# Projections of the next batch beside its first two score steps, and the weight shifts ten pieces later, in an attention and mixture-of-experts kernel

## The chip, the cores and the metric

The kernel runs on one core of a Trainium2 chip. The metric is the device time of one execution in microseconds (us); lower is better. The core has five engines that run their own instruction streams: TensorE (PE in the profile; its weight loads, PEld, are shown apart and overlap it), VectorE (DVE), ScalarE (ACT), GpSimd (POOL) and SyncE (SP), which here issues nearly all DMAs. Engines meet through semaphores; each executes its own stream in order, so an instruction that waits holds up all behind it.

## The reference, cut to what matters

The input x is 8 batches of 512 tokens of width 256. All is fp32.

```python
# attention, 16 heads of 16, causal; then residual and layer norm
q, k, v = split(x @ w_qkv);  a = softmax(mask(q @ k.T / 4)) @ v
x1 = layernorm(x + a @ w_out)
# feed-forward: top 6 of 16 experts by softmax(x1 @ gate_w.T) + gate_b
y = sum over chosen e of c[e] * (silu(x1 @ w1[e].T + b1[e]) * (x1 @ w3[e].T + b3[e]) @ w2[e].T + b2[e])
z = silu(x1 @ ws1.T + bs1) * (x1 @ ws3.T + bs3) @ ws2.T + bs2      # shared expert
out = layernorm(x1 + y + z)
```

## The kernel before, in words

**Batches and steps.** Each batch b goes through `attention(b)` (L332). Four first units prepare it: `transpose_x` (L337, 8 transposes on TensorE of the batch's tokens, tile x), `project_qk(0)` and `project_qk(1)` (L345, queries and keys of one half of the heads each) and `project_v` (L367). Then come 16 steps i, one for each of four query tiles q, two head halves m and two head parities s. Step i is in two parts: `front(i)` issues the score matmuls (sc, L399), whose results VectorE masks and reduces (L410) and GpSimd and ScalarE negate (L421, L426); `back(i)` turns the weights of step i-1 (transposes tp, L438, exponentials on ScalarE, L440) and adds up the weighted values of step i-2 (po, L447). So the pipeline is three steps deep, and two more units (16 and 17) empty it.

**Behind attention.** When a query tile is complete, `finish_tokens` (L478: output projection, residual, layer norm on VectorE), `transpose_tokens`, `gate`, `compare`, `place` and `send` follow at fixed distances of 3 to 15 pieces. `send` scatters the tokens on the GpSimd queue to the slots of their experts (xs). The shared expert of batch b is 7 units, `hidden` x3 and `collect` x4 (L655 to L712). `collect(t)` adds the shared result into the token tile x and then SyncE stores it (acc, L708).

**Groups.** Batches form three groups, (0,1), (2 to 5), (6,7). After the last batch of a group, `table(grp)` (L716) works out on VectorE which expert each tile of 128 slots belongs to, and then SyncE loads the ends of the experts from SBUF (L764) and issues 16 fills of the slots behind them (L772). `expert_units(grp)` (L795) then runs the routed experts a tile at a time; `fetch` brings the tokens (xg, L823), `up` and `down` are pab and py. Routed experts of one group run beside the attention of the next group.

**The order of the work.** It is written out by hand for TensorE, VectorE and ScalarE (`manual_schedule`, L1022). `line` (L959) is a list of pieces; for every piece the loop at L1023 issues what was put off to it (`due`), its own function, what lies beside it (`beside`, filled by `put`: clears, weight shifts, tables, expert units) and last its `behind`, here `back(i)`. Before the change a batch takes 20 pieces: 16 steps, unit 16 with the next batch's `transpose_x`, unit 17 with the next batch's `project_qk(0)`, and two pieces with nothing but `project_qk(1)` and `project_v` (L983, L984). The shared units of the batch before stand beside steps 7 to 13, and `load_x(b + 2)` beside step 14 (L974, L987). Expert units are spread evenly over the pieces of a group's stretch (L1018 to L1021). SyncE and GpSimd are not ordered by hand; a scheduler places their instructions.

**Token tiles.** `load_x` (L90) fills a tile from a pool of two. The load for batch b+2 writes into the tile of batch b, so it waits until the scatters of b have read it and until all four acc stores of b have read it. `transpose_x` of batch b+2 waits for the load; on TensorE everything behind it waits too.

**Weight shifts.** `shift_weights(e)` (L256) loads a correction for two experts (352 KB, L259, a pool of two buffers) and two and three pieces later adds it to the resident expert weights on VectorE (L263), 16 additions in all, from piece 22 on (L1006). The first routed expert runs at piece 63 before the change.

Of the kernel before, what the change touches and what calls it, by code (L numbers as in the profile page):

```python
# [31 lines left out]
def attn_moe_postln_kernel(  # L32
# [57 lines left out]
    def load_x(b):  # L90
        t = two.tile([P, NT, 2 * E + D], F32, tag="x", name=f"x_{b}")
        nc.sync.dma_start(out=t[:, :, 2 * E :], in_=x[b].rearrange("(t p) d -> p t d", p=P))
        xts[b] = t
# [162 lines left out]
    def shift_weights(e):  # L256

        c = two.tile([P, 2, 2 * EH], F32, tag="yg", name=f"shift_{e}")
        nc.sync.dma_start(out=c, in_=shift[e : e + 2].partition_broadcast(P))  # L259
        for i in range(2):  # L260
            w = wev[:, e + i, : 4 * EH].rearrange("p (c n) -> p c n", c=ND)
            ci = c[:, i].unsqueeze(1).to_broadcast([P, ND, 2 * EH])
            later(2 + i, lambda w=w, ci=ci: nc.vector.tensor_add(w, w, ci))  # L263
# [59 lines left out]
    def later(n, fn, last=False):  # L323
        due.setdefault(clock["now"] + n, ([], []))[last or n > 2].append(fn)
# [633 lines left out]
    parts = [attention(b) for b in range(B)]  # L958
# [5 lines left out]
    def add(fn, behind=nothing):  # L964
        line.append((fn, behind))
# [3 lines left out]
    rest = []  # L969
    for b in range(B):  # L970
        own = parts[b][1]
        for i, (fn, behind) in enumerate(own[:-2]):

            if i >= 7 and rest:  # L974
                add(lambda fn=fn, also=rest.pop(0): (fn(), also()), behind)
            else:
                add(fn, behind)

        nxt = parts[b + 1][0] if b + 1 < B else [nothing] * 4
        add(lambda a=own[-2][0], c=nxt[0]: (a(), c()), own[-2][1])  # L980
        add(lambda a=own[-1][0], c=nxt[1]: (a(), c()), own[-1][1])
        sent[b] = len(line) - 1 + 15
        add(nxt[2])  # L983
        add(nxt[3])  # L984
        rest = shared_units(b)
        if b + 2 < B:
            rest.append(lambda b=b: load_x(b + 2))  # L987
    for _ in range(14):
        add(nothing)
    for fn in rest:  # L990
# [7 lines left out]
    def put(at, fn):  # L998
        beside.setdefault(min(at, len(line)), []).append(fn)
# [3 lines left out]
        for i, b in enumerate(grp.batches):  # L1003
            put((sent[grp.batches[0]] if g else 30) + 12 * i, lambda b=b: clear(b))
    for e in range(0, E, 2):
        put(22 + e, lambda e=e: shift_weights(e))  # L1006
    for g, grp in enumerate(groups):
        put(starts[g], lambda grp=grp: table(grp))
        put(starts[g] + 2, lambda grp=grp: spread(grp))
# [83 lines left out]
```

## Time and profile before

| what | value |
|---|---|
| median of three runs | 1399.78 us (1398.6 to 1404.23) |
| the profiled execution: its own time | 1408.78 us |
| its span, first to last instruction | 1407.1 us |
| outside the span | 1.7 us |
| mean granted TensorE clock | 0.949 |
| busy: PE, POOL, DVE, ACT | 1310.7 us (93%), 890.1 (63%), 807.9 (57%), 713.5 (51%) |
| chain that ended last, by engine | PE 75%, DVE 8%, DMA 5%, SP's queue 4%, issue 3%, POOL 3%, ACT 2% |
| idle before scores' reduction e (L410), waiting for sc | 77.9 us of DVE |
| SP waiting for we_sb additions (L263) at L259 | 29.7 us |
| POOL waiting for the load of x at L370 | 15.4 us in 6 waits |

The page cuts the span in 40 slices of 35 us and gives the busy share of each in tenths, and in the row PEclk the clock that TensorE was granted. A view by windows gives the busy time of each engine, the clock and the DMA share in any stretch; the view in order of time gives each instruction's start and length, in square brackets the idle time just before it and what ended it. A matmul in fp32 is recorded as two instructions, so that four score matmuls show as x8.

### The profile page before, as it was taken

Reading aid. Unit: us, or ns where it says so; the run is one execution under the profiler, and the core shown is the slowest. Engines: PE = TensorE matmul, PEld = TensorE weight load, DVE = VectorE, ACT = ScalarE, POOL = GpSimd, SP = SyncE. Lnnn points to the kernel's source line nnn. Section 1 sums busy time; section 2 is a strip of 40 time slices with the busy share of each in tenths; the row PEclk is TensorE's granted clock in tenths of the full one; section 3 lists DMA queues with packets and bytes.
Section 4 is the critical chain, followed back from the end, with each engine's and each line's share of the span. In section 5 each row is a group of like instructions: output and inputs, shape, how many; then the busy total and the mean of one; then the engine's idle time right before and its main releaser. Section 6 shows DMA issues by size and latency. Waiting matters only on the chain.

```text
span 1407.1 us, 29371 instructions
## 1 busy us (share of the span) xinstructions
PE 1310.7 (93%) x8868; PEld 906.4 (64%) x8868; DVE 807.9 (57%) x2853; ACT 713.5 (51%) x1749; POOL 890.1 (63%) x1006
## 2 busy tenths in 40 slices
PE   7997998999999999999999999999989999999990
PEld 4564665666676577667756766677766765777770
DVE  3766967856664765666565844555534342255545
ACT  3442453454564455455555555555645554566660
POOL 3446647548656865775586557775567873577772
PEclk9995996999999999899999999999999999999995
DMA  9895211233223222333231345553456776587854
GB/s 279 230 348 175 69 53 51 72 105 84 62 54 88 56 68 65 72 76 68 56 89 45 102 103 96 94 113 68 83 107 131 136 146 130 125 157 167 176 120 138
DMA packets 184148, 156.73 MB, mean 111 GB/s; under 512 B 56109, under 2 KB 176570, under 8 KB 183994
## 3 DMA queue, kind: packets, MB, share of 16 engines
q1 hardware_dynamic: 140378, 100.51, 25.8%
q0 software_dynamic: 43344, 53.55, 21.2%
q8 instruction: 75, 1.23, 0.4%
q14 instruction: 79, 0.65, 0.2%
q10 hardware_dynamic: 272, 0.79, 0.1%
HBM read 66.08 MB, written 94.55 MB: 114 GB/s over the span
## 4 chain that ended last, share of the span: by engine, by line
PE 75%; DVE 8%; DMA 5%; SPq 4%; issue 3%; POOL 3%; ACT 2%; POOLq 0%; DVEq 0%; ACTq 0%; another core or an unknown queue 0%
PE pab L858 19%; PE py L878 14%; PE tp L438 8%; PE sc L399 5%; PE po L447 5%; PE tb L841 4%; PE tb L837 4%; PE qk L354 4%; PE pa L666 3%; SPq L311 3%; PE pb L666 2%; PE spy L698 2%; DVE e L410 2%; PE v L379 2%; PE pr L481 1%
## 5 line engine op out<-in xcount | busy, mean ns | idle before, releaser
L887 POOL DMA_INDIRECT sum<-y,yat x237 | 377.0, 1591 | 190.9 <-ACT y L886 112.2
L858 PE MATMUL pab<-we_sb,xgT 128*128 x936 | 325.6, 471 | 14.0 <-ACT xgT L848 8.1
L421 POOL TENSOR_SCALAR e<-e,nb 128x128 f32<-128x128 f32 (+3 forms) x384 | 222.1, 676 | 120.5 <-DVE nb L410 117.8
L410 DVE CUSTOM_DVE_ANT_0 e<-sc,none 128x512 f32<-128x512 f32 (+3 forms) x512 | 220.5, 485 | 84.9 <-PE sc L399 77.9
L878 PE MATMUL py<-we_sb,hT 88*128 (+1 forms) x948 | 249.8, 386 | 0.7 <-issue 0.5
L868 DVE SCALAR_TENSOR_TENSOR h<-h,pab 128x176 f32<-128x176 f32 x237 | 79.4, 335 | 279.8 <-ACT h L867 163.9
L878 PEld LDWEIGHTS py<-we_sb,hT 88*128 88x128 f32 (+1 forms) x948 | 183.4, 194 | 66.3 <-issue 5.0
L600 POOL DMA_INDIRECT xs<-x,idi x192 | 193.0, 1005 | 50.4 <-issue 44.7
L858 PEld LDWEIGHTS pab<-we_sb,xgT 128*128 128x128 f32 x936 | 162.7, 194 | 68.6 <-ACT xgT L848 9.7
L438 PE MATMUL tp<-ident,e 128*128 128x128 f32 x1280 | 183.5, 291 | 11.3 <-POOL e L421 5.2
L440 ACT ACTIVATE eT<-tp 128x512 f32<-128x512 f32 x320 | 170.7, 599 | 35.1 <-PE tp L438 30.7
L886 ACT ACTIVATE y<-py,yat 128x256 f32<-128x256 f32 x237 | 112.3, 474 | 132.3 <-PE py L878 98.3
L438 PEld LDWEIGHTS tp<-ident,e 128*128 128x128 f32 x1280 | 146.1, 147 | 45.3 <-issue 23.9
L399 PE MATMUL sc<-kT,qT 32*128 32x384 f32 (+3 forms) x1024 | 135.7, 511 | 9.6 <-DVE nb L410 7.4
L844 ACT COPY hT<-tb 88x256 f32<-88x256 f32 x237 | 87.2, 368 | 110.2 <-PE tb L841 85.5
L426 ACT ACTIVATE e<-e,nb 128x128 f32<-128x128 f32 (+3 forms) x128 | 71.2, 556 | 128.7 <-DVE nb L410 111.2
L867 ACT ACTIVATE h<-pab 128x176 f32<-128x176 f32 x237 | 75.1, 317 | 104.6 <-PE pab L858 82.2
L848 ACT ACTIVATE xgT<-tb,ident 128x256 f32<-128x256 f32 x234 | 110.9, 474 | 6.3 <-PE tb L841 2.1
L447 PE MATMUL po<-eT,v 128*32 128x128 f32 x2560 | 102.8, 289 | 11.1 <-DVE t L471 7.2
L447 PEld LDWEIGHTS po<-eT,v 128*32 128x32 f32 x2560 | 64.2, 112 | 56.3 <-issue 34.7
L837 PE MATMUL tb<-ident,h 128*88 128x128 f32 x474 | 92.8, 277 | 1.4 <-PE cnt L561 0.5
L841 PE MATMUL tb<-ident,xg 128*128 128x128 f32 x468 | 90.3, 275 | 3.5 <-DMA xg<-xs 3.4
(148 smaller groups left out, 1593.9 us busy)
## 6 DMA issues: line engine op xcount, KB each, us to landing
xg<-xs SPq DMA_DIRECT2D x237, 128.0 KB
sum<-none SPq DMA_DIRECT2D x24, 512.0 KB
yg<-sum SPq DMA_DIRECT2D x96, 128.0 KB
we_sb<-in_w SPq DMA_DIRECT2D x6, 1408.0 KB
xs<-none SPq DMA_DIRECT2D x3, 2304.0 KB
xs<-none SPq DMA_DIRECT2D x48, 144.0 KB
x<-in_x SPq DMA_DIRECT2D x8, 512.0 KB
acc<-x SPq DMA_DIRECT2D x32, 128.0 KB
```

The lines of the kernel that those rows point to most:

```text
L399: nc.tensor.matmul(sc[:, :n], lhsT=qT[ts(r, 32), m, s, ts(q, P)], rhs=kT[ts(r, 32), m, :n], start=True, stop=True,)
L410: nc.vector.tensor_tensor_reduce(out=e[:, :n], in0=scs[r][:, :n], in1=mask[:, S - n :], scale=-0.25, scalar=BIG, op0=ALU.add, op1=ALU.min, ...
L421: nc.gpsimd.tensor_scalar(e[:, :n], e[:, :n], -1.0, nb[:, r : r + 1], ALU.mult, ALU.add)
L438: nc.tensor.transpose(tp[:, ts(r, P)], es[r][:, ts(k, P)], ident)
L440: nc.scalar.activation(eT, tp, AF.Exp)
L447: nc.tensor.matmul(po[ts(r, 32), s, :], lhsT=v2[:, k, 4 * m + r, s : s + 2, :].rearrange("p h i -> p (h i)"), rhs=eTs[k][:, ts(r, P)], sta ...
L600: d = nc.gpsimd.indirect_dma_start(out=grp.xs, out_offset=bass.IndirectOffsetOnAxis(ap=idi[:, k : k + 1], axis=0), in_=xts[b][:, t, :], in ...
L837: nc.tensor.transpose(tp[:HC, 2 + c, :], h[:, ts(c, HC)], ident)
L841: nc.tensor.transpose(tp[:, c, :], xg[:, ts(c, P)], ident)
L858: nc.tensor.matmul(pab, lhsT=xgT[:, c, :], rhs=we_sb[:, ds(e * WE + c * 2 * EH, 2 * EH)], start=(c == 0), stop=(c == ND - 1),)
L878: nc.tensor.matmul(py, lhsT=hT[: HC + c, c, :], rhs=we_sb[: HC + c, ds(e * WE + 4 * EH + c * D, D)], start=(c == 0), stop=(c == 1),)
L887: nc.gpsimd.indirect_dma_start(out=grp.sums[j % SUMS], out_offset=bass.IndirectOffsetOnAxis(ap=st["at", j][:, 0:1].bitcast(I32), axis=0), ...
```

## The change

A batch now takes 18 pieces. `project_qk(1)` and `project_v` of batch b (b over 0) no longer have pieces of their own; they are issued right behind the score matmuls of that batch's steps 0 and 1. The shared units move from steps 7 to 13 to steps 6, 7, 8 (`hidden`) and 12, 13, 14, 15 (`collect`), and `load_x(b + 2)` is issued with the last `collect`, at step 15 in place of 14. The weight shifts start at piece 32 in place of 22. What is counted from the end of a batch (the `due` distances, `sent`, and so `table` and the first expert units) keeps its distance in pieces; since the two pieces are gone, it falls two steps later in the next batch: `table` at step 14 in place of 12, `send` of the last query tile at steps 12 to 14 in place of 10 to 12.

```diff
         for i, (fn, behind) in enumerate(own[:-2]):
 
-            if i >= 7 and rest:
+            if b and i < 2:
+                add(lambda fn=fn, also=parts[b][0][2 + i]: (fn(), also()), behind)
+
+            elif rest and (6 <= i < 9 or i >= 12):
                 add(lambda fn=fn, also=rest.pop(0): (fn(), also()), behind)
             else:
                 add(fn, behind)
...
         sent[b] = len(line) - 1 + 15
-        add(nxt[2])
-        add(nxt[3])
         rest = shared_units(b)
         if b + 2 < B:
-            rest.append(lambda b=b: load_x(b + 2))
+            rest[-1] = lambda b=b, fn=rest[-1]: (fn(), load_x(b + 2))
...
     for e in range(0, E, 2):
-        put(22 + e, lambda e=e: shift_weights(e))
+        put(32 + e, lambda e=e: shift_weights(e))
```

The compiled programs hold the same TensorE, VectorE, ScalarE and GpSimd work in another order; SyncE's DMAs are the same in number and size.

## The prediction

> **What bounds the kernel now.** I read the page first. TensorE is busy for 1310.7 of 1407.1 us and holds 75% of the chain that ended last. In the slices it is full except near the start and the end, and its clock drops to half twice near the start.
>
> ```profile
> PE   7997998999999999999999999999989999999990
> ...
> PEclk9995996999999999899999999999999999999995
> ```
>
> The fourth and seventh slices (105 to 140 and 211 to 246 us) are the first steps of batches 1 and 2. So I took the start of every score step from TensorE's instructions in order of time and asked the view by windows for steps 0 to 6 of each batch. Columns: stretch, length, busy PE, PEld, DVE, ACT, POOL, clock, DMA share, GB/s.
>
> ```profile
> 98.78:133.89 35.11, 22.60 (x152) 14.23 (x151) 25.95 (x104) 7.83 (x22) 23.04 (x35) 0.61 0.67 232
> 206.94:233.76 26.82, 21.84 (x151) 13.52 (x150) 20.86 (x96) 7.89 (x21) 20.92 (x35) 0.60 0.12 45
> 310.68:344.35 33.67, 32.27 (x213) 21.10 (x212) 24.42 (x109) 15.45 (x44) 26.06 (x38) 0.90 0.31 80
> 438.90:473.58 34.68, 31.53 (x224) 21.29 (x223) 24.87 (x108) 16.72 (x47) 29.51 (x40) 0.95 0.36 79
> 566.13:601.38 35.25, 32.66 (x224) 21.84 (x223) 24.81 (x108) 17.27 (x47) 29.99 (x39) 0.85 0.39 77
> 695.94:729.86 33.92, 31.59 (x224) 21.24 (x223) 24.49 (x107) 16.34 (x47) 28.63 (x38) 0.95 0.38 79
> 830.09:895.88 65.79, 62.63 (x379) 44.72 (x378) 33.73 (x140) 36.47 (x99) 53.16 (x58) 0.97 0.55 102
> ```
>
> Length less busy PE is the idle time: 12.5 us in batch 1, 5.0 in batch 2, then 1.4, 3.2, 2.6, 2.3, 3.2 (12.7) in batches 3 to 7. That is all that better cover in the first steps can win back, plus lost clock. The rest of each batch is TensorE-bound: in the window 310.70 to 438.90 us it is busy for 126.77 of 128.20 us. No matmul is removed, so the change pays only in waits, and any new wait of TensorE is paid in full.
>
> **Gains, part by part.** The weight shifts: the view in order of time shows VectorE stuck behind one load in batch 1:
>
> ```profile
> 119.61 0.89 DVE L263 TENSOR_TENSOR we_sb<-we_sb,shift 128x704 f32<-128x704 f32 x1 [5.69 <-DMA shift<-shift]
> ```
>
> TensorE waits 3.41 us for the division queued behind it. The load was issued at 106.6 us, while the clears and weight loads filled the DMA engines; ten pieces later that traffic is over, so the 3.4 us go. The 16 additions (0.89 us each in the median, 14 us) leave batch 1's early steps; some 7 of them, 6.2 us, arrive in steps 0 to 6 of batch 2, where VectorE is busy for 20.86 of 26.82 us and so has 6 us free: nearly full. The last addition comes at piece 49, the first expert at piece 61, so nothing routed waits for it.
>
> The projections: `project_qk(1)` took 3.70 us of TensorE, `project_v` 3.62 us, with nothing of their batch beside them. They now lie between the scores and the first transposes, where the waits for the chain reduction, negation, exponential stand (2.71 us on "DVE nb", 0.97 us on "POOL e" in batch 2). But they stand at steps 0 and 1 only; the waits of steps 3 to 6 stay, and the finishing work of the last query tile (about 3.5 us of VectorE) moves from steps 0 to 2 into steps 2 to 4. Bounds of the gain: nothing, and all the idle time. I take about half. Batch 1: 3.4, plus a third of the other 9.1, is 6.4 us. Batch 2: 2.5 less the additions, say 1. Batches 3 to 7: half of 12.7 is 6.3, and of the clock lost there ((1 - 0.90) x 33.7 + 0.05 x 34.7 + 0.15 x 35.3 + 0.05 x 33.9 + 0.03 x 65.8 = 14 us) a fifth, 3. Sum 16.7 us. Batches 1 and 2 without experts stay thin in steps 2 to 6, so I expect their clock to drop as now. The new copies of queries and values are the same instructions; on ScalarE they go ahead of step 0's last negation, and `project_v`'s 3.6 us of matmuls cover that; without this cover it would cost some 1 to 2 us a batch.
>
> **The cost: the load of the token tile.** This is the step I weigh most. Order on TensorE after the change, from the last `collect` (step 15) to the next batch's `transpose_x` (unit 16): counts, gate, at most one expert tile, po x32, tp x16, xp. In the trace of before the same stretch lasts 407.79 to 414.11 us, 6.3 us, with an expert tile, and 185.49 to 189.39, 3.9 us, without. Before, three steps lay between (`collect` at step 13).
>
> Against that stands the chain from the last spy matmul to the landed load. In the trace: VectorE adds (L706), SP stores (L708), the load (L92) is issued when that store has landed, and GpSimd's iota (L370) starts when the load has.
>
> ```profile
> 396.19 0.33 SPq L708 DMA_DIRECT2D acc<-x  x1
> 399.35 0.13 SPq L92 DMA_DIRECT2D x<-in_x  x1
> ...
> 404.30 0.19 POOL L370 IOTA x<- 128x64 int32 x1 [4.67 <-DMA yat<-xs]
> ...
> 414.11 1.04 PE L342 MATMUL xp<-ident,x 128*128 128x128 f32 x8
> ```
>
> The spy before it ended at 394.8, so the chain took 9.5 us; for the loads of batches 5, 6 and 2 it took 7.9, 8.7 and 8.5. Mean 8.7. Before, TensorE came to xp 15 to 20 us after spy, so nobody waited. Now it comes after 6.3 or 3.9.
>
> - Loads of batches 4, 5, 6 (an expert tile lies between): 8.7 - 6.3 = 2.4 each, 7.2 us. A rule of the Trainium skill gives less: "DMA: Bandwidth & Descriptors", section Anatomy of one DMA, puts a DMA at about 2.0 us plus its bytes at 436 GB/s, for the GpSimd path. By that the store (128 KB) is 2.3, the load (512 KB) 3.2, the chain with 1.4 us for the addition 6.9, and the stall 0.6 each. The trace has 1.9 to 3.2 and 4.0 to 5.4 for SP's own transfers beside other traffic; I take the trace.
> - Load of batch 2 (no expert tile): 8.7 - 3.9 = 4.8, plus a 352 KB weight shift that now stands just ahead of it on SP and waits for an addition of the same step; 0 to 3 us, I take 1. Sum 5.8.
> - Loads of batches 3 and 7: `table` now stands at step 14, and SP's order has the 16 fills ahead of the last store and of the load. In the trace:
>
> ```profile
> 274.52 0.15 DVE L758 SCALAR_TENSOR_TENSOR ends<-eio,run 1x16 int32<-1x16 f32 x1
> ...
> 275.98 9.37 SPq L772 DMA_DIRECT2D xs<-none  x15
> 285.45 0.39 SPq L708 DMA_DIRECT2D acc<-x  x1
> 287.37 0.39 SPq L92 DMA_DIRECT2D x<-in_x  x1
> ...
> 291.60 0.20 POOL L370 IOTA x<- 128x64 int32 x1 [1.30 <-DMA x<-in_x]
> ```
>
> From the ends to the landed load is 16.9 us, and the same from 784.8 to 801.7 for batch 7. Before, TensorE came to xp at 291.5 and 802.3: just in time, with `table` at step 12. Two steps later there is no slack. Step 14's reductions started 4.0 us after its scores on TensorE; with them, spy's addition and the table (2.5 + 0.4 + 3.5) the ends come 10.4 us after step 14's scores. TensorE needs 5.9 us from there to step 15's scores (sc 1.1, spy 1.4, x1p 0.4, po 1.0, tp 2.0), or 8.5 with an expert tile. So the ends come 4.5 us after step 15's scores in batch 2 and 1.9 in batch 6; the load lands at 21.4 and 18.8; xp is due at 1.1 + 1.4 + 3.9 = 6.4 and 8.8. Stalls 15 and 10 us; since VectorE may lag less, I take 14 and 10. The table's VectorE time falls in that shadow, which gives back about 3 us of waits in steps 13 to 15.
> - After two such stalls the clock may be cold. The one row for it is the start: after 7.06 us idle, xp took 1.94 us against 1.04, and 16 qk 8.13 against 7.30. That is 1.7 us a stall, 3.4 in all; at the least 0.
>
> Sum of costs: 7.2 + 5.8 + 24 + 3.4 = 40.4 us. Queued behind xp on TensorE are the output projection, po, the transposes of step 15 and `project_qk(0)`, so everything of the next batch waits; on SP the fetches of expert tokens queue behind the load, but they run three tiles ahead. The scatters of the old tile end well before (before: at step 10 to 12; now 12 to 14), so they aren't last.
>
> Expert tiles: the same number over 18 pieces a batch, 3.4 in place of 3.1 in a piece for the second group; TensorE-bound either way, 0. The tail after batch 7 keeps its order, 0, with 3 us of doubt either way.
>
> Net: 40.4 - 16.7 - 3 = 20.7 us slower. The profiled execution took 1408.78 us, 0.6% over the median of 1399.78; the difference is set against the median: 1420 us.
>
> **Rivals.** (a) The other side: the clock holds. If the dense projections at steps 0 and 1 keep TensorE at full clock through steps 2 to 6 of batches 1 and 2, then (1 - 0.61) x 35 + 0.40 x 27 = 24 us of lost clock come back besides the 17; with loads that land at the quick end (7.9) and smaller table stalls (8 each) the costs are 27. Then 1399.8 + 27 - 3 - 41 = 1383 us. It decides in favour of faster once batches 1 and 2 show a clock over 0.9 there. Against it: VectorE is 21 us busy in those steps without additions, so TensorE can't be dense. 7%. (b) No difference: stalls at the low end (27) against gains of 24 and the 3; 1400 us, 14%. (c) The stated cause, 1420 us, 65%. (d) Worse: the stalls leave the clock at half through the thin steps that follow, and the additions overload VectorE in batch 2; another 20 us, 1440, 14%.
>
> A measurement of this kernel can tell about 0.5%, 7 us, from no change. Faster 0.07, same 0.14, slower 0.79. The range reaches from the no-difference case to the worse one, 1399 to 1440 us.
>
> **What would show it.** TensorE idle before xp (L342) on the DMA of x: near 14 and 10 us for batches 3 and 7, 6 for batch 2, 2 to 3 for 4 to 6. The idle time in steps 0 to 6 down to 5 us in batch 1 and by half in batches 3 to 7, and no wait of L263 on the shift's load. I am wrong if xp doesn't wait, or if the clock of steps 0 to 6 in batches 1 and 2 rises above 0.9.

## The result, and the profile after

The changed kernel took 1473.67 us in the median of four runs (1471.05 to 1474.2), the kernel before beside it 1402.01 us: ratio 1.0508, interval 1.0475 to 1.054. The forecast was 1420 us with a range up to 1440: the direction was right, the size was not.

The page first, the two rows that were shown of before. The span is now 1471.7 us, so a slice is 37 us.

```profile
PE   7999979959999999899899969999999999999990
...
PEclk9998988879999999999999988999999999999995
```

The clock no longer falls to half in the early slices, but it stays at 8 and then 7 tenths in the sixth to ninth slice, where all but one were at 9 before; and PE has two slices at 5 and 6 tenths, the ninth (294 to 331 us) and the 24th (846 to 883), where batches 2 and 6 hand over to 3 and 7. Now the view by windows for steps 0 to 6 of batches 1, 2 and 4, with the columns of the earlier fence:

```profile
91.00:127.64 36.64, 32.20 (x197) 19.47 (x193) 21.76 (x103) 13.23 (x33) 21.84 (x37) 0.81 0.73 257
196.43:236.72 40.29, 32.90 (x197) 20.02 (x193) 27.06 (x109) 13.00 (x33) 22.96 (x37) 0.79 0.22 74
...
450.19:498.86 48.67, 44.97 (x280) 29.51 (x276) 28.71 (x121) 22.70 (x61) 31.52 (x43) 0.96 0.31 62
```

With 7.3 us more of projections in these steps, batches 1 and 2 hold a clock of 0.8 in place of 0.6. But length less busy PE is still 4.4 us in batch 1, and 7.4 and 3.7 us in batches 2 and 4, more than before. So I took the start of every step from TensorE's instructions in order of time and asked the view by windows for each stretch of batches 1 to 7. "Idle" is length less busy PE, "lost clock" is (1 - granted clock) x length; both in us, summed over the batches. Part of the time at a lower clock TensorE stood idle anyway, and that part would be counted twice. In brackets stands the clock lost while TensorE was busy, from the trace's clock records laid over its instructions; the difference is that of idle time and bracket.

| stretch | before: idle + lost clock (while busy) | after | difference |
|---|---|---|---|
| steps 0, 1 | 0.2 + 0.0 (0.0) | 19.0 + 10.2 (9.7) | +28.5 |
| steps 2 to 6 | 29.9 + 38.1 (31.6) | 17.6 + 20.5 (18.0) | -25.9 |
| steps 7 to 10 | 1.4 + 4.5 (4.5) | 1.8 + 1.7 (1.7) | -2.4 |
| steps 11, 12 | 0.0 + 0.0 (0.0) | 12.9 + 17.1 (16.4) | +29.3 |
| steps 13, 14 | 1.9 + 1.7 (1.7) | 0.0 + 0.0 (0.0) | -3.6 |
| step 15 to the next step 0 | 2.3 + 0.0 (0.0) | 30.3 + 11.9 (5.5) | +33.5 |
| from step 15 of batch 7 on | 48.7 + 22.3 (6.2) | 49.9 + 18.6 (1.7) | -3.3 |

The differences sum to 56.1 us of the 64.6 us by which the span grew. Sums of two terms further down, as in "19.0 + 10.2 us", are idle time and lost clock without the bracket. Three stretches lose. One of them, the load of the token tile, was forecast. The table's ends, the 16 fills, the load and TensorE's `transpose_x` for batch 3, in order of time:

```profile
290.18 0.15 DVE L758 SCALAR_TENSOR_TENSOR ends<-eio,run 1x16 int32<-1x16 f32 x1
291.10 9.39 SPq L772 DMA_DIRECT2D xs<-none  x16
...
302.51 0.39 SPq L92 DMA_DIRECT2D x<-in_x  x1
...
306.56 1.94 PE L342 MATMUL xp<-ident,x 128*128 128x128 f32 x8 [12.05 <-DMA x<-in_x]
```

The fills stand ahead of the load on SP, TensorE waits 12.05 us and its first transposes then run at half clock (1.94 us, later 1.06). The waits of all batches, from the view of waits by engine and line (us, times, longest):

```profile
PE xp L342 <- DMA x<-in_x: 37.5, 7, 12.1
```

Of the 37.5 us, 7.2 belong to batch 0's first load, which was there before.

The other two stretches were not forecast. The changed kernel's step 0 of batch 4, in order of time:

```profile
449.18 1.08 PE L447 MATMUL po<-eT,v 128*32 128x128 f32 x32
...
450.76 0.96 POOL L600 DMA_INDIRECT xs<-x,idi  x1 [0.30 <-issue]
...
454.35 0.62 ACT L461 ACTIVATE t<-po,par 128x128 f32<-128x128 f32 x2 [4.58 <-remote]
...
455.01 0.35 DVE L468 SCALAR_TENSOR_TENSOR t<-po,par,t 128x128 f32<-128x128 f32 x1 [4.98 <-ACT t L461]
...
457.41 0.42 PE L837 MATMUL tb<-ident,h 128*88 128x128 f32 x2 [2.68 <-DVE nb L410]
```

ScalarE's first copy for the division (L461) needs po and nothing else that is late; po ended at 450.26, and the copy starts at 454.35 ("remote" stands where the view can't name what ended a wait). In between, the last of six scatters run on GpSimd, one behind the other (444.37 to 451.72); they are those of the first query tile of batch 3. Behind L461 stand VectorE's division and step 0's reduction (L410), and behind that an expert tile on TensorE, which needs a PSUM bank that this reduction gives back: four banks hold the scores of step 0, two the queries and keys, one the transposed tokens, and there are seven. In steps 11 and 12 it is the same with the six scatters of the last query tile. Most of the table's 19.0 and 12.9 us of idle time are such waits. In batches 3, 4, 6 and 7 at step 0, and in batches 1 to 6 at steps 11 and 12, a stretch at half clock follows.

### The profile page after: what moved, and what is told of

Its sections match the earlier page's. It is cut to its first block, busy times and chain, and to the rows that moved or that the text cites. A ratio compares the mean times of both kernels' runs of the same rounds, so it can differ in the third digit from the quotient of the medians.

```text
span 1471.7 us, 29334 instructions
## 1 busy us (share of the span) xinstructions
PE 1328.1 (90%) x8868; PEld 915.2 (62%) x8868; DVE 807.3 (55%) x2853; ACT 716.7 (49%) x1749; POOL 886.3 (60%) x1006
## 4 chain that ended last, share of the span: by engine, by line
PE 77%; DVE 7%; DMA 4%; issue 4%; POOL 3%; ACT 2%; SPq 2%; another core or an unknown queue 1%; POOLq 0%; DVEq 0%; ACTq 0%
PE pab L858 18%; PE py L878 13%; PE tp L438 9%; PE sc L399 7%; PE po L447 5%; PE tb L837 3%; PE tb L841 3%; PE qk L354 3%; PE spy L698 3%; PE pa L666 3%; PE v L379 2%; PE pb L666 2%; DMA x<-in_x 2%; PE pr L481 2%; POOL xs L600 2%
## 5 line engine op out<-in xcount | busy, mean ns | idle before, releaser
L887 POOL DMA_INDIRECT sum<-y,yat x237 | 376.3, 1588 | 196.1 <-ACT y L886 152.1
L858 PE MATMUL pab<-we_sb,xgT 128*128 x936 | 321.6, 467 | 8.0 <-ACT xgT L848 4.5
L421 POOL TENSOR_SCALAR e<-e,nb 128x128 f32<-128x128 f32 (+3 forms) x384 | 216.2, 645 | 142.6 <-DVE nb L410 140.6
L410 DVE CUSTOM_DVE_ANT_0 e<-sc,none 128x512 f32<-128x512 f32 (+3 forms) x512 | 220.4, 485 | 72.4 <-PE sc L399 65.0
L438 PE MATMUL tp<-ident,e 128*128 128x128 f32 x1280 | 178.8, 286 | 8.4 <-POOL e L421 4.4
L886 ACT ACTIVATE y<-py,yat 128x256 f32<-128x256 f32 x237 | 112.2, 473 | 138.0 <-PE py L878 106.2
L837 PE MATMUL tb<-ident,h 128*88 128x128 f32 x474 | 92.6, 277 | 13.9 <-DVE nb L410 11.9
L447 PEld LDWEIGHTS po<-eT,v 128*32 128x32 f32 x2560 | 63.5, 111 | 53.6 <-issue 38.1
```

Source lines behind the costliest of these rows:

```text
L410: nc.vector.tensor_tensor_reduce(out=e[:, :n], in0=scs[r][:, :n], in1=mask[:, S - n :], scale=-0.25, scalar=BIG, op0=ALU.add, op1=ALU.min, ...
L421: nc.gpsimd.tensor_scalar(e[:, :n], e[:, :n], -1.0, nb[:, r : r + 1], ALU.mult, ALU.add)
L438: nc.tensor.transpose(tp[:, ts(r, P)], es[r][:, ts(k, P)], ident)
L447: nc.tensor.matmul(po[ts(r, 32), s, :], lhsT=v2[:, k, 4 * m + r, s : s + 2, :].rearrange("p h i -> p (h i)"), rhs=eTs[k][:, ts(r, P)], sta ...
L837: nc.tensor.transpose(tp[:HC, 2 + c, :], h[:, ts(c, HC)], ident)
L858: nc.tensor.matmul(pab, lhsT=xgT[:, c, :], rhs=we_sb[:, ds(e * WE + c * 2 * EH, 2 * EH)], start=(c == 0), stop=(c == ND - 1),)
```

## Experiments

Before is run beside every experiment on the same chip. Its own time differed from chip to chip: 1411 to 1413 us on two of six chips and 1383 to 1386 us on four. The runs below are told by chip, A and B for the two, C to F for the four; the pair of the forecast, with before at 1402 us and with the signs that are described below, behaves like A and B. A and B were used once each, so a property of the chip and one of its state on that occasion can't be told apart; D was used twice and was the same. The first four expectations were written without knowing this.

**The load alone (chip A).** Theory A: the waits for the token tile's load cost what they show. Rival B: the third tile brings everything back.

```diff
-        t = two.tile([P, NT, 2 * E + D], F32, tag="x", name=f"x_{b}")
+        t = three.tile([P, NT, 2 * E + D], F32, tag="x", name=f"x_{b}")
-            rest[-1] = lambda b=b, fn=rest[-1]: (fn(), load_x(b + 2))
+            rest[0] = lambda b=b, fn=rest[0]: (load_x(b + 2), fn())
```

The room comes from smaller pools elsewhere (y from six buffers to three, four small tiles from two to one).

> The changed kernel with a third token tile, so that the load for batch b+2 is issued at step 6 of batch b+1 and no longer waits for the last collect (to make room, the y tiles go from six to three and four small VectorE temporaries to one). By the accounts of the two traces the stretch from step 15 to the next batch grew by 28 us of idle TensorE and 12 us of lost clock. Theory A (several causes: the load, the scatters at step 11, the projections at step 0): the load's part goes, 1474 - 40 = 1434 us (1424 to 1446), no wait of xp on the load left, the idle time of steps 0 to 1 and 11 to 12 stays. Rival B (the load is the cause and the rest follows from it): about 1400 us.

1452.2 us, ratio 1.0309 (1.0251 to 1.0368). B falls. A's time is missed by 6 us, but this chip's before is 10.6 us slower than that of the forecast's pair; as a ratio A's range is 1.016 to 1.031, and the run lies at its upper end. The wait at xp is gone (7.3 us in one wait, batch 0's), and the stretch from step 15 on shows no idle and no lost clock and is 36.9 us shorter. Only 2.0 points of the ratio, some 28 us, came back, because the tail after batch 7 grew by 6 us and steps 0, 1, 11 and 12 by another 7. The stalls in steps 0, 1, 11 and 12 are all still there: 22.4 + 10.2 and 13.8 + 18.8 us.

**Other cover (chip A).** Two runs moved matmuls. In the first the four `collect` units stand at steps 9, 10, 11 and 15:

```diff
-            elif rest and (6 <= i < 9 or i >= 12):
+            elif rest and (6 <= i < 12 or i == 15):
```

> The changed kernel with collects 0, 1, 2 at steps 9, 10, 11 in place of 12, 13, 14; collect 3 and the load stay at step 15. Theory A: the six scatters that hold up GpSimd at step 11 find shared-expert matmuls beside them again; steps 11 and 12 lost 13 us idle and 17 us of clock, of which two thirds come back: 1453 us (1444 to 1464). Rival B (all from the load): 1474 us, within 5 us, since the load's chain isn't touched.

1477.1 us, ratio 1.0457 (1.041 to 1.0504): steps 11 and 12 lose 15.5 + 17.1 us as before. A miss: the `collect` beside step 11 did not cover the burst. In the second, `project_qk(1)` and `project_v` get their own pieces back, and the rest of the change stays:

```diff
-            if b and i < 2:
-                add(lambda fn=fn, also=parts[b][0][2 + i]: (fn(), also()), behind)
-            elif rest and (6 <= i < 9 or i >= 12):
+            if rest and (6 <= i < 9 or i >= 12):
...
+        add(nxt[2])
+        add(nxt[3])
```

> The changed kernel with the two projections back in pieces of their own (20 pieces a batch), with the new places of the shared units, the load at step 15 and the later weight shifts kept. The table is then at step 12 and the last scatters at steps 9 to 10 again. Theory A: what was lost at steps 0 and 1 (19 us idle, 10 us of clock) and what was gained at steps 2 to 6 (12 and 18 us) both go; the load still waits, but by about 2 to 4 us a batch without the table in front of it (15 us with the clock), and the scatters at step 9 stand without shared matmuls (10 us): 1425 us (1412 to 1438). Rival B: the load alone, 1402 + 12 = 1414 us.

1430.4 us, ratio 1.0129 (1.0084 to 1.0174). Steps 0 and 1 lose 1.6 us in place of 19.0 + 10.2, and steps 11 and 12 lose 1.2 in place of 12.9 + 17.1, since `send` stands two steps earlier again. But the burst is now at step 9, where `hidden` no longer lies beside it, and steps 7 to 10 lose 11.9 + 6.2 us. The stall goes with the burst of scatters to wherever it has no long matmuls beside it.

**The weight shifts alone (chip A):** before with `put(32 + e, ...)`.

> The kernel before with the weight shifts alone ten pieces later. Both theories: the wait of 5.7 us of VectorE in batch 1 goes, the additions land in batch 2: 1402 - 4 = 1398 us (1392 to 1404). A rival says that the additions in batch 2 hold up VectorE: 1406 us or more, and then a part of the loss of the change is the shifts'.

1405.79 us, ratio 0.996 (0.994 to 0.9981). As expected: some 5 us of gain, and none of the cost.

**Later projections, later hidden units, split bursts (chip C).** Three runs were to tell apart what makes steps 0 and 12 wait. S: the position (no cover, no free PSUM bank). R: the length of the burst.

```diff
-            if b and i < 2:
-                add(lambda fn=fn, also=parts[b][0][2 + i]: (fn(), also()), behind)
+            if b and 1 <= i < 3:
+                add(lambda fn=fn, also=parts[b][0][1 + i]: (fn(), also()), behind)
```

> The changed kernel with the second half of the projections beside steps 1 and 2 in place of 0 and 1. Theory S (step 0 loses because its four score banks, two query banks and the token transposes fill all seven PSUM banks while the scatters of the first query tile run, so that an expert tile waits for a bank): by step 1 the banks are free again; of the 19 us idle and 10 us of lost clock in steps 0 and 1 most goes: about -22 us, ratio about 1.035. Rival R (the scatter burst itself holds up the engines, whatever is beside it): the loss moves to steps 1 and 2, -5 to +5 us, ratio 1.046 to 1.055.

```diff
-            elif rest and (6 <= i < 9 or i >= 12):
+            elif rest and i >= 9:
```

(This kernel also has a second buffer for the transposed tokens and the smaller pools of the first run.)

> The changed kernel with the shared expert's hidden units beside steps 9, 10, 11 (collects at 12 to 15 as they are), which needs two buffers for the transposed tokens; smaller pools elsewhere make the room. Theory S (the scatters of the last query tile now run at step 11 where no 3.6 us block of shared matmuls lies): idle 12.9 and lost clock 17.1 us of steps 11 and 12 go, up to 5 us come back at steps 6 to 8, net about -22 us, ratio about 1.035. Rival R (the block does not cover the 5 to 7 us for which the burst holds things up): at most -5 us, ratio 1.047 or more.

```diff
-            later(2, lambda: keep(t, all3))
+            later(2, lambda: keep(t, all3, 0))
+            later(4, lambda: keep(t, all3, 3))
...
-                for i in range(3):
-                    later(13 + i, lambda i=i: send(q, 2 * i))
+                later(13, lambda: send(q, 0))
+                later(15, lambda: send(q, 3))
```

(`keep` and `send` handle three slots from the given one on.)

> The changed kernel with the slots of a query tile worked out in two halves, two pieces apart, so that its scatters come as two bursts of three in place of one of six (32 x 2 small VectorE instructions more, 0.1 to 0.2 us each). Theory R (the length of the burst is what stalls steps 0 and 11 to 12): a burst of three lasts 3.7 us and TensorE has about that much queued; the losses of these steps (19 + 10 and 13 + 17 us) fall by half or more: -30 us, ratio about 1.03. Rival S (what lies beside the steps matters, not the burst): -5 to +5 us, ratio 1.046 to 1.055.

They took 1403.93 us, ratio 1.0133 (1.011 to 1.0157); 1418.48 us, ratio 1.025 (1.0227 to 1.0272); and 1384.54 us, ratio 0.9991 (0.9979 to 1.0004). All three lie below what either theory forecast; by themselves the first two speak for S and the third for R. But the second run leaves steps 0 and 1 as the change has them, and they lost nothing in it: 0.0 + 0.0 us. So the ratios of this chip can't be set against 1.0508, and the changed kernel had to be measured on such a chip.

**The changed kernel on another chip (chip D).** No edit.

> The changed kernel once more, unaltered, on the chip on which the next three run. In the runs with the projections later, the hidden units later and the scatters split, TensorE's steps 0 and 1 show no idle time at all, although one of them left these steps as they were; so part of the loss there may belong to the chip. If steps 0 and 1 depend on the chip, ratio 1.02 to 1.04 on a chip like theirs and 1.05 on one like the earlier ones; if they don't, 1.05 on any.

(In one point this expectation misreads its runs: the one with later projections did lose 4.1 + 6.8 us in steps 0 and 1.)

1391.71 us against 1385.73, ratio 1.0037 (1.0024 to 1.0051). The same program costs 5 per cent on one chip and less than half of one on another. Here is the same place of batch 4 as above, in order of time:

```profile
425.25 1.08 PE L447 MATMUL po<-eT,v 128*32 128x128 f32 x32
...
426.39 0.62 ACT L461 ACTIVATE t<-po,par 128x128 f32<-128x128 f32 x2 [0.57 <-PE po L447]
...
426.83 0.96 POOL L600 DMA_INDIRECT xs<-x,idi  x1 [0.30 <-issue]
...
430.44 0.38 PE L837 MATMUL tb<-ident,h 128*88 128x128 f32 x2
```

The six scatters are as long as before (0.96 to 1.00 us each) and stand at the same place (420.44 to 427.79); the copy L461 starts 0.06 us after po's end in place of 4.09, and the expert tile waits for nothing. Step 11 of batch 3 shows it too. First the changed kernel in the first measurement, then on chip D, in order of time:

```profile
394.54 1.53 PE L438 MATMUL tp<-ident,e 128*128 128x128 f32 x12
...
398.88 0.62 ACT L461 ACTIVATE t<-po,par 128x128 f32<-128x128 f32 x2 [4.05 <-PE sc L399]
399.40 1.57 ACT L440 ACTIVATE eT<-tp 128x512 f32<-128x512 f32 x3
...
400.05 1.77 PE L399 MATMUL sc<-kT,qT 32*128 32x512 f32 x2 [2.00 <-ACT eT L440]
```

```profile
377.50 1.53 PE L438 MATMUL tp<-ident,e 128*128 128x128 f32 x12
377.70 0.61 ACT L461 ACTIVATE t<-po,par 128x128 f32<-128x128 f32 x2
378.20 1.58 ACT L440 ACTIVATE eT<-tp 128x512 f32<-128x512 f32 x3
...
378.96 1.14 PE L399 MATMUL sc<-kT,qT 32*128 32x512 f32 x8
```

From 388 us to the start of tp the two executions run in step to 0.02 us (offset 17.02 to 17.04); then ScalarE, which waits for TensorE's results, goes on 4.1 us later in the first. The trace also records each update of a semaphore. In the first trace TensorE's updates stop at 392.96 us, in the middle of the burst. The one due at 393.82 has no record, but ScalarE's L886, which waits for it, runs at 393.85. The next seven, due from 394.61 to 398.05, are recorded from 398.86 to 399.17, some 0.05 us apart: they were held and then came out together.

Counted as gaps are stretches of over 2 us without an update in which at least two were due. There are 44 in the first trace of the changed kernel, 34 in that of before, and none in the trace of chip D, nor in any other of chips C to F. Of the 44, 20 end with two or more updates less than 0.1 us apart; the rest end with a single one and may only be missing records. The nine that end with six or more all lie over the bursts of six in step 11 and around step 0 of batches 3 to 7. ScalarE's and VectorE's semaphores have 57 and 16 gaps in the same trace, and each ends with a single update: for these engines it shows missing records, but no held updates.

The view by windows of batch 4 (steps 0 and 1; steps 11 and 12; step 15 to the next step 0), first measurement, then chip D:

```profile
450.20:469.50 19.30, 16.59 (x83) 11.22 (x79) 6.65 (x32) 6.49 (x17) 7.13 (x11) 0.91 0.22 43
526.10:547.80 21.70, 20.05 (x131) 13.02 (x130) 11.14 (x38) 8.09 (x21) 14.33 (x18) 0.84 0.24 67
563.70:589.40 25.70, 23.04 (x207) 16.76 (x206) 11.53 (x39) 14.39 (x33) 12.69 (x15) 1.00 0.31 76
```

```profile
426.30:440.90 14.60, 14.60 (x86) 10.42 (x82) 6.65 (x32) 6.64 (x17) 7.13 (x11) 1.00 0.30 57
497.00:511.40 14.40, 14.40 (x129) 10.39 (x128) 11.27 (x37) 8.04 (x21) 12.37 (x16) 1.00 0.36 101
527.80:552.80 25.00, 23.02 (x207) 16.72 (x207) 11.54 (x39) 13.84 (x32) 12.71 (x15) 1.00 0.33 78
```

4.7 and 7.3 us of the first two stretches are gone, the third (the load) is nearly as it was. Against 1.0037 the two runs with later projections and later hidden units are 1.0 and 2.1 points worse. With later projections steps 0 to 6 of batches 1 to 7 take 308.7 us, against 294.9 on chip D. With later hidden units steps 7 to 10 are bared (13.6 + 3.7 us, against 1.8 + 1.7), and the tail, with the smaller pools, is 12.3 us longer. They say nothing on the stall, since their chip doesn't show it. Three more kernels ran on chip D: the changed kernel with split bursts, before with split bursts, and split bursts with the third tile.

> The changed kernel with its scatters in bursts of three, beside the unaltered one on the same chip. If the burst's length is the cause of the losses in steps 0, 1, 11 and 12: at least 25 us below the changed kernel, ratio at most 1.03 wherever that has 1.05. If the earlier equality with before came from the chip alone: within 8 us of the changed kernel.

1385.09 us, ratio 0.9998 (0.9986 to 1.0011), 6.6 us under the changed kernel: where updates are prompt, splitting is worth half a per cent in the changed kernel.

> The kernel before with its scatters in bursts of three, nothing else. If bursts are covered there by the projections' own pieces and the hidden units, as its trace suggests (no idle time in steps 9 and 0 to 1): ratio 0.99 to 1.00. If bursts cost the kernel before as much as the changed one: 0.96 to 0.97, and the change itself would then still cost 3 to 5 per cent.

1391.65 us, ratio 1.0043 (1.0013 to 1.0073): the kernel before becomes 0.4 per cent slower by it, and its steps 0 and 1 show 8.0 us of idle time. It was not run where updates come late.

> Third token tile and scatters in bursts of three, with the projections beside steps 0 and 1 as in the change. Against the run that had these two and the projections at steps 1 and 2 (0.975 of before): the same within 0.5 per cent if the burst was what stalled step 0; slower by 1 per cent or more if the full PSUM banks of step 0 matter by themselves.

1351.63 us, ratio 0.9747 (0.9719 to 0.9775). Against the split bursts alone the third tile takes 33.5 us; its stretch had shown 30.8 + 13.7 us (6.6 while busy) and is 38.2 us shorter, and the tail, with the smaller pools, is 8.8 us longer. A run on chip C had these two and the projections at steps 1 and 2:

> Three cures in one: a third token tile (loaded at step 6), projections at steps 1 and 2, and scatters in bursts of three. If the three losses are all there is and the cures don't disturb one another, the wait for the tile (30 us idle, 12 us of lost clock), step 0 (29) and steps 11 and 12 (30, of which half) go: about -80 us against the changed kernel, some 1395 us, ratio about 0.995. If the clock that was lost merely moves to other stretches as in the run with the third tile alone: -50 us, ratio about 1.015.

1349.65 us, ratio 0.975 (0.9726 to 0.9773): the same within the intervals. With split bursts and prompt updates the place of the projections doesn't matter; what full PSUM banks do where updates come late, these two runs don't test.

**Do split bursts cure it where updates come late?** Bursts of three were run again, on chips as they came. (In the next expectation "the run above" is the one on chip E of the last pair below.)

> The changed kernel with scatters in bursts of three, on the same chip as the run above. Where the updates come late: ratio 1.00 to 1.02 if bursts of three cure it, 1.04 to 1.06 if not. Elsewhere 1.00.

> As before: the changed kernel with scatters in bursts of three, on a chip as it comes. Where TensorE's updates come late (before at 1400 us or more): ratio 1.00 to 1.02 if bursts of three cure it, 1.04 to 1.06 if not. Elsewhere 1.00.

On chips E and D: 1387.57 us, ratio 1.0013 (1.0002 to 1.0025), and 1386.42 us, ratio 1.0007 (0.9992 to 1.0021). Nothing new; both chips are prompt. The third pair fell on chip B, where before took 1410.93 us:

> The third token tile alone once more, on a chip as it comes. Where TensorE's updates come promptly, the changed kernel stands at 1.004 of before, and the wait for the tile (30 us idle, 12 us of lost clock) is all that the third tile takes away: ratio 0.975 if all of it comes back as time, 0.99 if half of it reappears elsewhere, as it seemed to in the first run with a third tile. Where they come late: 1.03 again.

> The changed kernel with scatters in bursts of three, on the same chip as the run above. Where TensorE's updates come late: ratio 1.00 to 1.02 if bursts of three cure it, 1.04 to 1.06 if not. Elsewhere 1.00.

The third tile with bursts of six took 1452.36 us, ratio 1.0304 (1.0264 to 1.0343), the bursts of three with two tiles 1410.5 us, ratio 1.0001 (0.9976 to 1.0025), on one chip. In the first, steps 0 and 1 lose 22.5 + 11.9 us and steps 11 and 12 lose 13.9 + 17.1; in the second 1.3 + 0.0 and 3.1 + 0.0. The same place of batch 4 with bursts of three on chip B, in order of time:

```profile
429.36 1.08 PE L447 MATMUL po<-eT,v 128*32 128x128 f32 x32
...
431.54 0.63 ACT L461 ACTIVATE t<-po,par 128x128 f32<-128x128 f32 x2 [1.60 <-PE sc L399]
```

L461 is 1.10 us behind po's end: still late, but with enough queued on TensorE to hide it. The trace even has more gaps (57, of which 30 end in a row of updates), some of them beside a single indirect DMA of L887. But in batches 1 to 6 the oldest update due in a gap is at most 3.1 us late, against up to 7.6 in the first trace of the changed kernel. The two runs also differ in the third tile, which on chip A left the stalls of steps 0, 1, 11 and 12 as they were. So the burst's length is the cause there, and what the change added is cured. It is not all that late updates cost: these 1410.5 us are still 23 to 26 us over the same program on chips C, D and E, and before is slower there by as much.

**The version that beats both,** split bursts and third tile, on two more chips, E and F:

> Third token tile and scatters in bursts of three once more, on a chip as it comes. Theory C (on some chips TensorE's semaphore updates come out 4 to 6 us late while six scatters run back to back, and only there does the change cost 5 per cent): on such a chip before takes 1400 us or more, and with bursts of three the late updates are gone, ratio 0.96 to 0.98; on another chip before takes some 1386 us and the ratio is 0.975 again. If bursts of three don't help on such a chip: ratio 1.00 to 1.03 there, as with the third tile alone (1.031).

> Third token tile and scatters in bursts of three, on a chip as it comes; on two chips with prompt updates it took 0.975 and 0.978 of before. On a chip with late updates, bursts of three brought the changed kernel to 1.000 of before and the third tile takes 2 per cent off the changed kernel, so 0.98; with prompt updates 0.975 again. If the two cures overlap on a chip with late updates: 0.99 to 1.00.

1353.76 us, ratio 0.9781 (0.9763 to 0.9799), and 1350.94 us, ratio 0.9769 (0.9751 to 0.9787). On a chip with late updates it wasn't run; each of its two cures was, by itself.

## Why the prediction was wrong

**The load of the token tile: right in its mechanism, somewhat too large.** Predicted were 40.4 us with the cold clock; the stretch lost 33.5 us more than before. Term by term the idle time was 12.0 us for batch 3 (14 predicted), 8.7 for batch 7 (10), 3.2 for batch 2 (5.8), 2.2, 2.6 and 1.5 for batches 4 to 6 (2.4 each): 30.3 for 37. The cold clock cost 5.5 us while TensorE was busy, for 3.4: one row of half-speed transposes at the start was too little to size it.

**The gains: too small.** Predicted were 16.7 and 3; steps 2 to 6 gave 25.9, steps 7 to 10 2.4 and 13 to 14 3.6, 31.9 us in all. No L263 waits for its shift any more. Of the 25.9 us 13.6 are clock: in steps 0 to 6 of batches 1 and 2 it went from 0.6 to 0.8. That is part of rival (a), whose clock of over 0.9 wasn't reached. These two parts alone sum to 33.5 - 31.9 = 1.6 us slower; on chip D, where the scatters stall nothing, the changed kernel costs 6 us of 1386.

**The step that failed** is the one on the projections at steps 0 and 1, with its last sentence: `project_v` covers what goes ahead on ScalarE, and "without this cover it would cost some 1 to 2 us a batch"; the sum took 0. It cost 28.5 us, 4.1 a batch. With it goes what had no term at all: the `hidden` units leave the steps at which the last query tile's scatters run, and the burst moves from step 9 to step 11. That was 29.3 us. The working looked at the scatters only as readers of the token tile ("so they aren't last"), not at who works beside them. In the profiled executions 64.6 us stand against the 20.7 us of the sum, so 43.9 are missing. The two stalls make 57.8; the gains set too low by 12.2 and the load set too high by 6.9 leave 38.7 of them. The other 5.2 us are not broken down.

The trace of before held the warning. Its unit 17 of batch 3, in order of time:

```profile
424.78 1.08 PE L447 MATMUL po<-eT,v 128*32 128x128 f32 x32
...
430.68 0.62 ACT L461 ACTIVATE t<-po,par 128x128 f32<-128x128 f32 x2 [5.32 <-PE tb L841]
```

po ended at 425.86 and ScalarE took it up 4.8 us later, while six scatters ran (420.59 to 428.00). Nothing showed as idle time of TensorE, because 7.3 us of projections in their own pieces, which wait for nobody, were queued there. At step 9 `hidden` did the same: before loses nothing to speak of in steps 7 to 10, and the run with own pieces, without `hidden` there, lost 11.9 + 6.2 us. What looked like two pieces of plain work was the cover of a stall, and the change took both covers away. Projections "with nothing of their batch beside them" were read as work to be put beside something else, without asking what it already stood beside on GpSimd.

**What the runs showed of it and what not.** Shown: the stall goes with bursts of six scatters without long matmuls beside them (own pieces on chip A; bursts of six and of three on chip B), it appears on some chips only (the same program on chip D), and bursts of three bring the time back. The PSUM banks are how step 0's wait reaches TensorE, not its cause: on chip D the same tiles hold the same banks and nothing waits. Not settled: why TensorE's updates come late, whether by the chip or by its state on the day, and whether the recording takes part. The changed kernel without a cure was not run on chips A and B beside the others; the pair of the forecast and the runs with a third tile stand for it.

**Rivals.** "No difference" is what chip D shows for the change as a whole, and there the load still waits 30.1 us, so not by the smaller stalls that this rival supposed. "Worse" had the right sign with another mechanism. That the forecast of "slower" came true owes something to luck: on chip D the 20.7 us of the sum would have been too many.

## What to carry to other kernels

Before moving a block of matmuls, list what runs beside it on every engine at that moment, bursts of indirect DMAs on GpSimd above all: a block that waits for nothing may be what hides somebody else's delay. Keep such bursts short (three in place of six cost two small VectorE instructions a tile here) and give a tile whose load waits for late readers one more buffer; together they took 2.2 to 2.5 per cent off the kernel before on three chips, all with prompt updates. And when a result is far from a sum whose parts check out, run the unaltered kernel on another chip before building theories on it.

## What the hardware showed

- On two of six chips, and in the pair of the forecast, TensorE's semaphore updates are held during back-to-back indirect DMAs of GpSimd and then come out together. In the places shown, ScalarE's L461 starts 4.1 to 4.8 us behind po with six scatters, 1.1 us with three, and 0.06 us on chip D, with scatters of the same 0.96 to 1.00 us. The traces with late updates also lack records: in the first trace of the changed kernel 1794 of 1933 updates of TensorE's semaphore and 1333 of 1594 of ScalarE's are there, in that of chip D 1929 and 1581. The Trainium skill, "NOTIFIC — the notification-queue block", section Overflow: three behaviours, one of which stalls the engine, says that a full queue of records can, in one of three settings, hold up the engine that makes them, so the recording itself may take part; no run here tests that.
- The kernel before is 2 per cent slower on such chips (1411 to 1413 us against 1383 to 1386).
- Short idle times of TensorE cost as much again in clock. In steps 11 and 12, 12.9 us of idle time in seven batches went with 16.4 us of clock lost while it was busy. In batches 1 to 6, whose longest waits there are 1.0 to 3.1 us, the granted clock fell to half for 3.41 or 6.83 us; in batch 7, after a wait of 0.74 us, it did not.
